# Routing's two small products ahead of image 0's last three w1 products, ternary and bias steps behind its weighted tiles

## The chip, the cores and the metric

The kernel runs on one core of a Trainium2 chip. The core has a matrix engine (PE, with its weight loads shown apart as PEld), a vector engine (DVE), an activation engine (ACT), a general engine (POOL), and a queue engine (SP) from which almost all transfers here are issued. Each engine works through its own instructions in order and waits on semaphores for the others. The metric is the device time of one execution in microseconds. Before the change the median of three runs was 3424.55 us, from 3424.52 to 3428.01 us. All data are float32.

## The reference, cut to what matters

Four layers are applied in turn to x of shape 8 x 384 x 32 x 32: a convolutional attention block, a gated mixture of four experts, a ternary depthwise and pointwise convolution, and a deformable attention block. The change touches the second layer and the preparation of the third layer's weights.

```
scores = softmax(x_flat @ gate_w + gate_b)         # 4 experts
top_v, top_i = top_k(scores, 2)
top_w = softmax(top_v)
wmap = top_w.T.reshape(K, b, h, w)                 # by position in the flat list
present = (top_i[:, :, None] == arange(e)).any(0)  # over all tokens
coef = einsum('ke,kbhw->ebhw', present, wmap)
hdn = relu(einsum('bchw,edc->ebdhw', x, w1) + b1)
y   = einsum('ebdhw,eod->ebohw', hdn, w2) + b2
out = einsum('ebohw,ebhw->bohw', y, coef)

# third layer: weights made ternary, then two convolutions
scale = 1 / max(mean(abs(w)), 1e-5)
u = clip(round(w * scale), -1, 1)
```

Which experts are present is a maximum over all tokens of all images, so nothing can be weighted before every token has been routed. The weighting is linear in one number per token: with w0 the first choice's weight, an expert's coefficient is dp x w0 + p1, where p1 says whether the expert is anybody's second choice, and dp is "anybody's first choice" less p1.

## The kernel before, in words

Each image is held as 128 partitions x 3 channel blocks x 1024 tokens and handled in two halves of 512 tokens. [...] a float32 product shows as two passes in the profile.

The stretch of interest lies between the first layer and the pipelined loop over images. There, image by image, the first layer's output is joined and the gate logits are accumulated (`logits`, L1239). Between these, PE takes the first products of layer 2 for image 0, whose list of units `layer1(pl, 0, True)` (called late) makes:

- 24 units of `hidden` (L1493): for each half and each of 12 hidden tiles, three products with w1; ACT then applies bias and relu (L1503) to a tile named hd (first half) or hx (second half). In the late form the tiles are not weighted at once.
- 24 units of `result`: for each half, each of 3 output blocks m and each of 4 parts, three products with w2 (L1514) that accumulate in one bank y. With the first four units (half 0, m = 0) go the weights of half 0's tiles, with the next four (half 0, m = 1) those of half 1's: ACT makes a coefficient tile cb from the broadcast weight w0s (L1475), and DVE multiplies each hidden tile by it (`weight`, L1479). After the last part DVE adds y to the image (L1520).
- The bias step (`bias`, L1466) adds w0 x yb to the image in three DVE operations per half; it is called ahead of the weights.

`route` (L1255 on) turns the logits by products with sel2 (L1263), has DVE and ACT work out the softmax, the two maxima, the presence pres and the weight w0 (L1272 to L1324), then takes all w1 units still left off the list, and then has PE do two small products: ppres sums pres over all partitions (L1313), and w0t turns w0 (L1327). DVE makes prs and w0r of them (L1317, L1329). w0r is stored to DRAM (w0d, L1330), from where `spread` loads it broadcast over all partitions (w0s, L1457). This load waits for the store. `coefficients` makes dp and yb.

`weights23` loads the third layer's weights pw2 and dw2 into raw (L1354, L1355), makes them ternary on DVE (tap2 small, upw2 128 x 1152), with one product pm on PE (L1380) that sums the magnitudes mp (L1378), and prepares two small vectors. It is called after the ninth result unit.

Order on an engine follows a scheduler, which may place an instruction ahead of others traced before it. `tc.issue_after(ins)` holds the instructions traced in its block behind `ins` on that engine. Before the change weights23 is held behind w0r's copy. Image 1's x loads (L171) and o loads (L1425) are issued from SP in the same stretch. Banks of PSUM for these products come from `fbank`, three in turn.

Of the kernel before, what the change touches and what calls it, by code (L numbers as in the profile page):

```python
# [9 lines left out]
ALU = mybir.AluOpType  # L10
# [4 lines left out]
P = 128  # L15
KC = C // P
# [17 lines left out]
NE = 4  # L34
# [21 lines left out]
def tile_kernel(ctx: ExitStack, tc: tile.TileContext, i: dict, out: bass.AP):  # L56
    nc = tc.nc
# [97 lines left out]
    def bn_moments(st, j, tiles):  # L155

        return nc.vector.bn_aggr(tiles[0][:, j, :], st[:, j, :, :].rearrange("p a b -> p (a b)"))
# [109 lines left out]
    with ExitStack() as pa:  # L267
# [46 lines left out]
        ident = const.tile([P, P], F32, name="ident_sb")  # L314
# [103 lines left out]
        first = [[w[0] for w in work].index(u) for u in range(NU0)]  # L418
# [103 lines left out]
        for n, (u, kind, s) in enumerate(work):  # L522
            k, h = divmod(u, 2)
# [19 lines left out]
            if n == len(work) - 2:  # L543
                spread = spread_qk()
# [8 lines left out]
            if kind == "v":  # L553
                h, c = h + s, 0
# [5 lines left out]
            for p in passes:  # L560
                j, x = p
                c0, c1 = max(0, 1 - x), W - max(0, x - 1)
                for q in range(nq):
# [3 lines left out]
                    elif kind == "y":  # L567
                        g, j, w = s, q, slice(0, 64)
# [103 lines left out]
    with ExitStack() as pb:  # L672
# [195 lines left out]
        for n, (b, pr, h, kc) in enumerate(steps):  # L868
# [49 lines left out]
            if kc == NT8 - NS:  # L918
                turned = normalise(b, pr, h, pav)
# [14 lines left out]
        for m in range(KC):  # L934
            first = bn_moments(ost, m, sc_o)
# [72 lines left out]
    with tc.If(redo > 0):  # L1008
        with ExitStack() as pb:
# [13 lines left out]
            with tc.For_i(0, B) as bi:  # L1023
# [44 lines left out]
                for pr in range(NPAIR0):  # L1068
                    qt, kt = qks[0][:, pr, :], qks[1][:, pr, :]
                    for h in range(2):  # L1070
                        pav = bank(f"pav_e{pr}_{h}")
                        for j, r in enumerate(HR):
                            hd = 2 * pr + j
# [73 lines left out]
    def load_w(name):  # L1147
        src = i[name]
        t = wd.tile(list(src.shape), F32, tag=name, name=name + "_sb")
        nc.sync.dma_start(out=t, in_=src)  # L1150
        return t
# [8 lines left out]
    def fbank(name):  # L1160
        return ps_f.tile([P, HALF], F32, tag="f", name=name)
# [93 lines left out]
    def route(units, end):  # L1255


        ls = pl.one([P, HALF], "ts", "ls")
        nc.vector.tensor_copy(ls, plog)

        pt = fbank("plt").rearrange("p (q a b e) -> p q a b e", q=8, a=2, b=B)
        for q in range(4):
            nc.tensor.matmul(  # L1263
                pt[:, q].rearrange("p a b e -> p (a b e)"), lhsT=ls[:, q * P : (q + 1) * P],
                rhs=sel2, start=True, stop=True,
            )
        nc.tensor.matmul(
            pt[:, 4, 0].rearrange("p b e -> p (b e)"), lhsT=ones,
            rhs=tb.rearrange("p b e -> p (b e)"), start=True, stop=True,
        )  # L1270
        gb = wd.tile([P, B, NE], F32, name="gb")
        nc.vector.tensor_tensor(  # L1272
            gb, pt[:, 4, 0], gbias.unsqueeze(1).to_broadcast([P, B, NE]), ALU.add
        )
        nt = B * NT8
        lg = pl.one([P, B, NT8, NE], "vt", "lg")
        for a in range(2):
            for q in range(4):
                nc.vector.tensor_tensor(lg[:, :, 4 * a + q, :], pt[:, q, a], gb, ALU.add)
        l = lg.rearrange("p b t e -> p (b t) e")  # L1280
        wk = pl.one([P, 3, nt, NE], "kt", "routing")
        wv = pl.one([P, 5, nt], "om2", "routed")

        def bc(ap):
            return ap.unsqueeze(2).to_broadcast([P, nt, NE])

        sc, eq, oh = (wk[:, k] for k in range(3))
        m = wv[:, 4]
        nc.vector.reduce_max(m, l, AX.X)
        nc.vector.tensor_tensor(l, l, bc(m), ALU.subtract)  # L1290
        nc.scalar.activation(sc, l, AF.Exp)
        nc.vector.reduce_sum(m, sc, AX.X)
        nc.vector.reciprocal(m, m)
        nc.vector.tensor_tensor(sc, sc, bc(m), ALU.mult)
        tops = []
        for k in range(2):
            mk, ek = wv[:, 2 * k], wv[:, 2 * k + 1]
            nc.vector.reduce_max(mk, sc, AX.X)

            nc.vector.tensor_tensor(eq, sc, bc(mk), ALU.is_equal)  # L1300
            nc.vector.tensor_tensor(
                eq, eq, ewt.unsqueeze(1).to_broadcast([P, nt, NE]), ALU.mult
            )
            nc.vector.reduce_max(ek, eq, AX.X)
            nc.vector.tensor_tensor(oh, eq, bc(ek), ALU.is_equal)
            nc.vector.reduce_max(pres[:, k, :], oh.rearrange("p t e -> p e t"), AX.X)
            if k == 0:
                nc.vector.scalar_tensor_tensor(sc, oh, -2.0, sc, ALU.mult, ALU.add)
            tops.append(mk)
        while len(units) > end:  # L1310
            units.pop(0)()
        pp_ = fbank("ppres")
        nc.tensor.matmul(  # L1313
            pp_[:, : 2 * NE], lhsT=ones, rhs=pres.rearrange("p k e -> p (k e)"),
            start=True, stop=True,
        )
        nc.vector.tensor_scalar(  # L1317
            prs.rearrange("p k e -> p (k e)"), pp_[:, : 2 * NE], 0.0, None, ALU.is_gt
        )
        nc.vector.tensor_tensor(m, tops[1], tops[0], ALU.subtract)  # L1320
        nc.scalar.activation(m, m, AF.Exp)
        nc.vector.tensor_scalar(m, m, 1.0, None, ALU.add)
        w0f = w0.rearrange("p b t -> p (b t)")
        nc.vector.reciprocal(w0f, m)  # L1324

        wt = fbank("w0t")
        nc.tensor.transpose(wt[:nt, :P], w0f, ident)  # L1327
        wr = pl.one([P, HALF], "ts", "w0r")
        routed = nc.vector.tensor_copy(wr[:nt, :P], wt[:nt, :P])  # L1329
        nc.sync.dma_start(out=w0_dram.rearrange("b (t p) -> (b t) p", p=P), in_=wr[:nt, :P])  # L1330
        return routed

    prs = wd.tile([P, 2, NE], F32, name="prs")
    dp = wd.tile([P, NE], F32, name="dp")
# [74 lines left out]
    ahead = {"time": 0.0}  # L1409
# [5 lines left out]
    def layer1(pl, b, late=False):  # L1415
# [11 lines left out]
        state = {}  # L1427
# [35 lines left out]
        def bias(h):  # L1463
            hs = slice(h * HALF, (h + 1) * HALF)
            for m in range(KC):
# [2 lines left out]
                    ALU.mult, ALU.add,  # L1468
                )

        def weight(h, k):
            e, dc = divmod(k, KC)
            if dc == 0:
                cb = state["cb"] = pl.one([P, HALF], "cb", f"cb{b}_{h}_{e}", 2)
                nc.scalar.activation(  # L1475
                    cb, state["w0", h], AF.Identity, bias=p1[:, e : e + 1], scale=dp[:, e : e + 1]
                )
            hd = state[h, k]
            nc.vector.tensor_tensor(hd, hd, state["cb"], ALU.mult)  # L1479

        def spare(k):

# [43 lines left out]
        units = []  # L1526

        def unit(*calls):
            units.append(lambda: [f(*a) for f, *a in calls])

        if late:
            for h in range(2):
                unit((enter, h), (hidden, h, 0))
                for k in range(1, NE * KC):
                    unit((hidden, h, k))
            for h in range(2):
                for m in range(KC):
                    for part in range(4):

                        w, n = (0, part) if h == m == 0 else (1, 4 * m + part - 4)  # L1540
                        first = []
                        if n == 0:
                            first += [(spread, w), (bias, w)]
                        if h == 0 and n < 4:
                            first += [(weight, w, 3 * n + k) for k in range(3)]
                        unit(*first, (result, h, m, part))
            return units
        spread(0)
# [616 lines left out]
    units = layer1(pl, 0, True)  # L2165
# [4 lines left out]
    for b in range(1, B):  # L2170
# [8 lines left out]
        if b + 2 == B:  # L2179
            with tc.issue_after(ahead["load"].ins):  # L2180
# [1 line left out]
                wq3, wk3, wv3, wp3 = (load_w(n) for n in ("wq3", "wk3", "wv3", "wp3"))  # L2182
                pb3, dw3, bn3, pw3 = (load_w(n) for n in ("pb3", "dw3", "bn3", "pw3"))
                ref3, npos, half3, same = (load_w(n) for n in ("ref3", "npos", "half3", "same"))
    routed = route(units, 2 * NE * KC)
    coefficients()
    with pd:
        for k, u in enumerate(units):
            u()
            if k == 8:  # L2190
                with tc.issue_after(routed.ins):
                    tap2, upw2, mp, so3, bo3, sum2, edge2 = weights23(pl)
        def layers(b):
            xt = xs_img.pop(b)
            yield from layer2(pl, b, xt)
            yield from layer3(pl, b, xt, put_image(b), False)

        for b in range(B - 1):
            units = layer1(pl, b + 1)
            due = 0.0  # L2200
            this = layers(b)
            for idle in this:
                if idle is None:
                    if b == B - 2:
                        break
                    continue
                due += idle
                while due >= UNIT and units:
                    units.pop(0)()
                    due += ahead["time"] - UNIT  # L2210
                    ahead["time"] = 0.0
            if b == B - 2:
                for _ in range(5):
                    next(this)
            for u in units:
                u()

        def fill(n):
            for _ in range(n):
                next(this, None)  # L2220

        for _ in last_image(pl, xs_img.pop(B - 1), fill):
            pass
        in_range(slice((B - 2) * NU3, B * NU3), 1)
        okm = pl.one([P, 1], "okm", "okm3")
        nc.vector.tensor_reduce(okm, oks, AX.X, ALU.min)
        pok = fbank("pok3")
        nc.tensor.matmul(pok[:, 0:1], lhsT=ones, rhs=okm, start=True, stop=True)
        nc.vector.tensor_scalar(bad3, pok[:, 0:1], P - 0.5, None, ALU.is_lt)
# [164 lines left out]
```

## Time and profile before

| What | Value |
|---|---|
| Median of three runs | 3424.55 us |
| Profiled execution: its own time | 3426.77 us |
| Profiled execution: span | 3424.7 us |
| PE busy | 3325.3 us (97%) |
| DVE busy | 1776.0 us (52%) |
| ACT busy | 1300.0 us (38%) |
| POOL busy | 203.7 us (6%) |
| w1 products, PE, L1493 | 1104 recorded, 597 ns each |
| w2 products, PE, L1514 | 1080 recorded, 599 ns each |
| cb, ACT, L1475 | 797 to 815 ns each |
| weighted tiles, DVE, L1479 | 684 ns each |
| mean granted PE clock | 0.989 |

A row of the profile names the line, the engine, the operation, and the tiles written and read. "<-" in a wait names what ended it. Matmuls overlap, so the start-to-start time, about 0.43 us a pass in this stretch, tells PE's rate better than the duration of one. Times of a stretch are us from the start of the span. The granted clock is a share of full speed; half rate is 0.50.

### The profile page before, as it was taken

The page shows a single profiled execution, that of the slowest core. Times are in us where ns is not written, and L with a number is a line of the kernel's source. Part 1 is how long each engine was busy: PE and PEld are TensorE (multiplying, and loading weights), DVE is VectorE, ACT ScalarE, POOL GpSimd, SP SyncE. Part 2 cuts the span into 40 slices and gives each one's busy share as a digit, 9 for nine tenths or more (in the row PEclk, how much of TensorE's full clock was granted, in tenths as well). Part 3 has the DMA queues.
Part 4 walks back from the last instruction along what each step waited for, and adds up shares of the span by engine and source line. Part 5 has one row for each costly group of instructions (what it writes and reads, how often), then busy time and mean ns, then how long its engine had stood idle before and what let it go on. Part 6 is the DMA issues. An engine that isn't in the chain of part 4 may idle for free.

```text
span 3424.7 us, 44837 instructions
## 1 busy us (share of the span) xinstructions
PE 3325.3 (97%) x18479; PEld 1440.2 (42%) x18479; DVE 1776.0 (52%) x2982; ACT 1300.0 (38%) x1519; POOL 203.7 (6%) x237
## 2 busy tenths in 40 slices
PE   6999999999999999999889999999999999999989
PEld 2443434343434343434334444444444444444444
DVE  8852232323232323234456586565855658658765
ACT  5655444444444444434212332223322232222341
POOL 2110000000000000000000110201102011020121
PEclk9999999999999999999899999999999999999999
DMA  9972121212121211112810110101101011010000
GB/s 354 295 226 81 27 80 27 81 26 80 27 73 34 65 43 58 50 57 63 304 41 22 36 40 26 60 28 36 40 30 56 28 36 40 36 55 23 0 19 38
DMA packets 86980, 234.56 MB, mean 68 GB/s; under 512 B 21881, under 2 KB 22105, under 8 KB 79851
## 3 DMA queue, kind: packets, MB, share of 16 engines
q1 hardware_dynamic: 84602, 223.30, 20.3%
q10 hardware_dynamic: 1248, 4.72, 0.4%
q8 instruction: 149, 2.44, 0.3%
q0 software_dynamic: 912, 3.53, 0.3%
q14 instruction: 69, 0.56, 0.1%
HBM read 146.33 MB, written 75.59 MB: 65 GB/s over the span
## 4 chain that ended last, share of the span: by engine, by line
PE 49%; DVE 1%; DMA 1%; ACT 0%; POOL 0%; issue 0%; SPq 0%; DVEq 0%; POOLq 0%; ACTq 0%
PE ph L1493 15%; PE y L1514 14%; PE pf L2022 4%; PE pq L1674 3%; PE pw L1645 3%; PE pav L1894 3%; PE s L1868 2%; PE pk L1839 1%; DVE off L1770 1%; PE pv L1850 1%; PE xsb L1820 1%; PE pw_last L2083 1%; PE xs L1820 0%; PE px L1734 0%; PE plog L1239 0%; PE pom L1701 0%
## 5 line engine op out<-in xcount | busy, mean ns | idle before, releaser
L827 ACT ACTIVATE p<-s 128x1024 f32<-128x1024 f32 x512 | 496.3, 1021 | 365.7 <-PE s L820 365.5
L1493 PE MATMUL ph<-h,w_sb 128*128 128x512 f32 x1104 | 487.9, 597 | 14.7 <-DMA b_sb<-in_b_dram 14.6
L1514 PE MATMUL y<-hd,w_sb 128*128 128x512 f32 x1080 | 487.4, 599 | 11.1 <-DVE hd L1479 11.1
L835 PE MATMUL pav<-p,vt 64*64 64x512 f32 x4096 | 494.7, 588 | 0.0
L820 PE MATMUL s<-qk,qk 48*64 48x512 f32 x2944 | 355.2, 592 | 0.0
L1493 PEld LDWEIGHTS ph<-h,w_sb 128*128 128x128 f32 x1104 | 208.4, 191 | 272.3 <-issue 269.8
L1514 PEld LDWEIGHTS y<-hd,w_sb 128*128 128x128 f32 x1080 | 200.0, 191 | 242.7 <-issue 222.6
L796 DVE COPY ta<-pav 128x512 f32<-128x512 f32 (+1 forms) x65 | 44.2, 682 | 475.5 <-PE pav L835 475.5
L835 PEld LDWEIGHTS pav<-p,vt 64*64 64x64 f32 x4096 | 168.3, 133 | 273.7 <-issue 273.4
L1503 ACT ACTIVATE hd<-ph,b_sb 128x512 f32<-128x512 f32 x180 | 122.6, 681 | 265.1 <-PE ph L1493 265.1
L574 PE MATMUL pk<-xs,cws_sb 32*32 32x496 f32 (+3 forms) x3840 | 182.9, 614 | 37.8 <-DMA xs<-in_xs_dram 24.6
L1770 DVE SCALAR_TENSOR_TENSOR off<-q,dw_sb,off 128x225 f32<-128x225 f32 (+4 forms) x441 | 215.3, 541 | 2.6
L1633 DVE SCALAR_TENSOR_TENSOR y<-h,tap,y 128x961 f32<-128x961 f32 (+1 forms) x168 | 202.9, 1227 | 0.5
L820 PEld LDWEIGHTS s<-qk,qk 48*64 48x64 f32 x2944 | 109.4, 133 | 211.2 <-issue 190.3
L81 DVE COPY qk<-pq 128x512 f32<-128x512 f32 x46 | 31.8, 691 | 251.9 <-PE pq L258 251.9
L1885 ACT ACTIVATE p<-s 128x1024 f32<-128x1024 f32 x96 | 93.4, 1021 | 162.0 <-PE s L1868 152.6
L1479 DVE TENSOR_TENSOR hd<-hd,cb 128x512 f32<-128x512 f32 x180 | 122.2, 684 | 37.8 <-ACT hd L1503 37.5
L574 PEld LDWEIGHTS pk<-xs,cws_sb 32*32 32x32 f32 (+1 forms) x3840 | 78.8, 112 | 140.4 <-issue 57.3
L1954 POOL TENSOR_TENSOR p<-p,p 128x1024 f32<-128x1024 f32 x48 | 113.6, 2367 | 325.9 <-ACT p L1885 267.1
L2022 PE MATMUL pf<-att,wp_sb 128*128 128x512 f32 x288 | 131.3, 601 | 0.0
L820 PE MATMUL s<-ql,ql 48*64 48x512 f32 x1024 | 128.2, 592 | 0.2 <-ACT p L827 0.2
L711 PE MATMUL pv<-wv_sb,g 128*128 128x384 f32 x384 | 127.1, 489 | 0.0
(369 smaller groups left out, 3745.2 us busy)
## 6 DMA issues: line engine op xcount, KB each, us to landing
rqk<-y SPq DMA_DIRECT2D x96, 256.0 KB
g<-rqk SPq DMA_DIRECT2D x96, 256.0 KB
xs<-in_xs_dram SPq DMA_DIRECT2D x56, 384.0 KB
g<-rv SPq DMA_DIRECT2D x48, 256.0 KB
xh<-in_x_dram SPq DMA_DIRECT2D x48, 256.0 KB
f<-in_x_dram SPq DMA_DIRECT2D x24, 512.0 KB
f<-o SPq DMA_DIRECT2D x24, 512.0 KB
o<-ot SPq DMA_DIRECT2D x42, 256.0 KB
```

What stands on the lines that cost most here:

```text
L574: nc.tensor.matmul(banks[r][cols[q]].rearrange("p (h w) -> p h w", w=W)[:, :, c0:c1], lhsT=cws[rs, c, 2 * h + g, x, w], rhs=src[rs, :, c0 ...
L711: nc.tensor.matmul(pv[:, :C], lhsT=acts[b][2][:, c, t * P : (t + 1) * P], rhs=w_in[2][:, c, :], start=(c == 0), stop=(c == KC - 1),)
L820: nc.tensor.matmul(s[64 * k : 64 * k + 64, j * HALF : (j + 1) * HALF], lhsT=kt[r, k0 : k0 + 64], rhs=qt[r, h * HALF : (h + 1) * HALF], sta ...
L827: nc.scalar.activation(p, s, AF.Exp, scale=scale)
L835: nc.tensor.matmul(pav[k][64 * j : 64 * j + 64, :], lhsT=vts[b % 2][r, kc, 2 * hd : 2 * hd + 2, :].rearrange("p a b -> p (a b)"), rhs=p[r, ...
L1479: nc.vector.tensor_tensor(hd, hd, state["cb"], ALU.mult)
L1493: ahead["ph"] = nc.tensor.matmul(ph, lhsT=w1[:, e, c, dc * P : (dc + 1) * P], rhs=state["h1"][c], start=(c == 0), stop=(c == KC - 1),)
L1503: nc.scalar.activation(hd, ph, AF.Relu, bias=b1[:, k : k + 1])
L1514: nc.tensor.matmul(y, lhsT=w2[:, e, dc, m * P : (m + 1) * P], rhs=state[h, k], start=(k == 0), stop=(k == NE * KC - 1),)
L1633: nc.vector.scalar_tensor_tensor(d, f, tap2[:, c, t : t + 1], d, ALU.mult, ALU.add)
L1770: nc.vector.scalar_tensor_tensor(d, f, dw3[:, t : t + 1], d, ALU.mult, ALU.add)
L2022: nc.tensor.matmul(pf, lhsT=wp3[:, pr, m * P : (m + 1) * P], rhs=att[:, pr, hs], start=(pr == 0), stop=(pr == NPAIR3 - 1),)
```

## The change

One edit is on PE's order and two are on DVE's. In `route`, the loop that takes the remaining w1 units stops three units short; these three come after the turning product w0t, held behind it on PE. In the late units of image 0, `bias` goes from the head of the first part to a call `late_bias` after the weights of the fourth part, held behind the last weighted tile so far. `weights23` is held behind the last weighted tile traced when it is called, not behind w0r's copy.

```diff
-        while len(units) > end:
+        while len(units) > end + 3:
             units.pop(0)()
         pp_ = fbank("ppres")
...
-        nc.tensor.transpose(wt[:nt, :P], w0f, ident)
+        turned = nc.tensor.transpose(wt[:nt, :P], w0f, ident)
         wr = pl.one([P, HALF], "ts", "w0r")
-        routed = nc.vector.tensor_copy(wr[:nt, :P], wt[:nt, :P])
+        nc.vector.tensor_copy(wr[:nt, :P], wt[:nt, :P])
         nc.sync.dma_start(out=w0_dram.rearrange("b (t p) -> (b t) p", p=P), in_=wr[:nt, :P])
-        return routed
+        with tc.issue_after(turned.ins):
+            while len(units) > end:
+                units.pop(0)()
...
+        def late_bias(h):
+            with tc.issue_after(ahead["hd"].ins):
+                bias(h)
...
-            nc.vector.tensor_tensor(hd, hd, state["cb"], ALU.mult)
+            ahead["hd"] = nc.vector.tensor_tensor(hd, hd, state["cb"], ALU.mult)
...
                         if n == 0:
-                            first += [(spread, w), (bias, w)]
+                            first += [(spread, w)]
                         if h == 0 and n < 4:
                             first += [(weight, w, 3 * n + k) for k in range(3)]
+                        if n == 3:
+                            first += [(late_bias, w)]
                         unit(*first, (result, h, m, part))
...
-    routed = route(units, 2 * NE * KC)
+    route(units, 2 * NE * KC)
...
-                with tc.issue_after(routed.ins):
+                with tc.issue_after(ahead["hd"].ins):
                     tap2, upw2, mp, so3, bo3, sum2, edge2 = weights23(pl)
```

On the SP queue the order changes with it. Before: pw2, dw2 and two of image 1's three x loads, then the store of w0d, the third x load, and the broadcast load w0s. After: the store of w0d, pw2, w0s, dw2, and then the three x loads.

## The prediction

> **What bounds the kernel now.** I read the page's busy shares first: PE is busy for 3325.3 of 3424.7 us (97%), DVE for 52%, ACT for 38%. So PE's own stream sets the time, and a change can gain only what PE idles or runs slowly. The view of waits, for PE, from 1700 us to the end, lists where PE still waits (columns: waiting engine and line, what it waited for, us in total, times, longest us):
>
> ```profile
> PE y L1514 <- DVE hd L1479: 11.1, 1, 11.1
> PE pav L1894 <- DVE tu L1966: 5.4, 1, 5.4
> PE pw_last L2083 <- ACT y_last L2075: 3.3, 1, 3.3
> ```
>
> The first line is one single wait, the largest left after 1700 us, and it lies exactly where the diff edits. To see what fills it I took the chain that ended last, in order of time, for 1680 to 1800 us (start, duration, what):
>
> ```profile
> 1702.43 18.11 PE ph L1493 x42
> 1720.54 0.14 PE ppres L1313 x2
> ...
> 1720.69 0.17 DVE prs L1317
> 1720.86 0.26 DVE w0r L1329
> ...
> 1721.53 2.43 DMA w0d<-w0r
> ...
> 1724.03 5.12 DMA w0s<-w0d
> ...
> 1729.17 2.08 DVE f L1466 x3
> 1731.25 0.61 DVE hd L1479
> ...
> 1731.91 25.45 PE y L1514 x54
> ```
>
> PE runs all its w1 products, then the two small products (ppres, w0t). Only then can the routing weight go through DRAM: copy w0r, store w0d, broadcast load w0s, bias steps, first weighted tile hd. All that time PE has nothing. Was the input of the small products ready earlier? The timeline of instructions answers:
>
> ```profile
> 1712.37 0.51 DVE L1306 TENSOR_REDUCE pres<-routing 128x4 f32<-128x256 f32 x1
> 1712.65 1.02 PE L1493 MATMUL ph<-h,w_sb 128*128 128x512 f32 x2
> 1720.37 0.28 PE L1313 MATMUL ppres<-pres,ones 128*128 128x8 f32 x2
> 1720.57 0.69 ACT L1503 ACTIVATE hx<-ph,b_sb 128x512 f32<-128x512 f32 x1 [1.83 <-PE ph L1493]
> ```
>
> pres was complete at 1712.88 and w0's reciprocal (L1324) at 1712.45. The matmul at 1712.65 is the first of the last three w1 units. So the products waited 7.5 us behind three units that do not need them.
>
> The wait has a second price. The table by stretches (columns: stretch, length, busy us and count of PE, PEld, DVE, ACT, POOL, then granted clock, DMA share, GB/s) shows PE's clock falling during it:
>
> ```profile
> 1724.00:1725.00 1.00, 0.00 (x0) 0.00 (x0) 0.93 (x9) 0.00 (x0) 0.00 (x0) 1.00 0.72 287
> 1727.00:1728.00 1.00, 0.00 (x0) 0.00 (x0) 0.00 (x0) 0.00 (x0) 0.00 (x0) 0.50 0.83 336
> 1730.00:1732.00 2.00, 0.09 (x1) 0.10 (x1) 2.00 (x4) 0.77 (x2) 0.00 (x0) 0.50 0.00 0
> ```
>
> The clock records put the half rate at 1725.74 to 1735.98 us. The y products therefore start slowly: 54 passes took from 1731.91 to 1757.19, or 25.28 us. At the 0.4287 us a pass of the w1 stream (1712.65 to 1720.37 holds 18) they need 23.15. Lost: 2.13 us.
>
> [...] half rate starts 4.9 us after PE stopped and lasts 10.24 us. [...] Here the 32 KB store took 2.43 us, [...] the trace shows cb behind the last hx on ACT, and I use that below.
>
> **The change part by part.** The clock starts at 1712.65, where PE is ready for the first of the last three units.
>
> (1) Products ahead of the last three units. They wait for pres: 1712.88 plus 0.05 (hd's end to PE's load at 1731.9 took that). From ppres to the end of prs took 1720.86 - 1720.37 = 0.49; with a weight load ahead, some 0.6. In the changed program's order the next w1 product takes ppres's PSUM bank and so waits for prs. I put its start at 1713.6, that is 0.95 late. Of this, 0.42 (1720.37 to 1720.79) is the products' own time, paid before too. New PE loss: 0.53. Bounds: 0.2 and 1.2. Behind this wait on PE stand only the three units. They end at 1713.6 + 18 x 0.4287 = 1721.32.
>
> (2) The DRAM chain. w0r ended 0.74 after ppres began, so now at about 1713.05 + 0.74 = 1713.8. From w0r's end (1721.11) to cb's start (1729.26) the path took 8.15, so w0s is usable at 1721.95. On the SP queue two things change. The 576 KB load of pw2 was far ahead; now it is issued between w0d and w0s. It replaces a 512 KB load of x in the same place, so I take the same time. The rest of image 1's x and dw2 go behind w0s, and x is first used near 1791, some 65 us later. Bounds of the chain: 0.5 us faster, 3 us slower if pw2 and x's loads share the engines with w0s worse than x did.
>
> (3) ACT. cb stands behind the last hx. PE's end to hx's end was 1720.37 to 1721.26 = 0.89, so hx ends at 1722.21. That is later than w0s's 1721.95: the two nearly tie, and ACT decides. cb starts at 1722.25 and takes 0.81.
>
> (4) Bias moved behind the weighted tiles. The first hd no longer waits for three L1466 steps. They ended at 1731.25 while cb was ready near 1730.07, so this alone is worth 1.1 us. Now hd: 1723.06 + 0.05 + 0.68, and y starts at 1723.84. PE idles 1723.84 - 1721.32 = 2.52 us. The bias is then needed by y's first addition (L1520), about 10 us after y starts, while DVE needs 7.3 + 2.1 us for twelve hd and three bias steps: no wait on PE, as the bank y leaves is one of three.
>
> (5) Ternary steps moved behind the weighted tiles. Before, the small ones lay in DVE's idle time (1721.1 to 1726.2), costing nothing; now neither, with one cover to watch: pm on PE, the sum of pw2's magnitudes, stands after 54 y passes, at 1723.84 + 23.15 = 1747.0, and needs mp (1.33 us). DVE reaches mp after 24 weights (about 14.7 us), six bias steps (4.2), one y addition (0.75) and a 0.17 reduction: 1723.1 + 19.8 + 1.33 = about 1744.3. Slack 2.7 us. The large steps (upw2, some 5 us) follow pm as before, long ahead of the first use in image 0's pointwise product.
>
> (6) [...] the half rate should not come: 2.13 us saved.
>
> Sum: before 11.12 + 2.13 = 13.25 lost; after 0.53 + 2.52 = 3.05. Gain 10.2 us. After this stretch the order on every engine is the same, and PE is at 100% from 1800 to 3200 (0.06 to 0.22 us missing in some stretches), so what PE gains it keeps. The profiled execution took 3426.77, which would become 3416.6; the median of the three runs is 3424.55, which becomes 3414.4. Those runs spread over 3.5 us, one at 3428.01; [...] I allow 2 us either way.
>
> **The rivals.** R1, a late transfer takes the wait over: w0s comes 2 to 4 us later since pw2 lies ahead of it. For: its slack against ACT is 0.3 us, and w0s's packets were already slow (5.12 us for 512 KB). Against: x's load lay in the same place before. The gap becomes about 5.3 us at 3 us late, the clock can fall again, and the gain shrinks to 5.5 to 7.5: 3417.0 to 3419.1. R2, the gain is given back at image 1's start: PE waited only 0.88 there (ph after h L1443), but its o loads are issued only when image 0's last y products free buffers. If those loads had a fixed time, 3424.5. Against: that issue is tied to PE's own progress and moves with it. R3, slower: pm. If DVE reached mp late, PE, in order, would stand before it with the y products behind. It costs from 2.7 us of lateness on, and the kernel is slower once DVE is over 2.7 + 10.2 = 13 us late, for example 20 us late: 3431.7. For: mp now stands behind some 20 us of DVE work. Against: the durations are measured and DVE is idle for 4.6 and 8.8 us in that stretch before.
>
> **How the numbers follow.** About 0.2% (6.85 us, 3417.7) is what a measurement can tell from no change. Forecast 0.83, with its own range 3412 to 3417; R1 0.10, half of it beyond 3417.7; R2 0.04; R3 0.03. Faster 0.83 + 0.05 = 0.88, same 0.05 + 0.04 = 0.09, slower 0.03. The range runs from 1's best bound with a favourable tail, 3411.6, to most of R1, 3418.6.
>
> **What would show it.** Right: ppres near 1713, PE's wait before y at 2 to 3 us and put down to hd, no half-rate record there, y starting near 1723.8, pm with no wait. Wrong: cb starting well after the last hx, released by w0s (R1); a wait before pm (R3); a larger wait at ph or x of image 1 (R2); or PE idling over 1.2 us before ppres.

## The result, and the profile after

The changed kernel took 3416.61 us (median of 8 runs, 3414.96 to 3421.18). The kernel before, run beside it, took 3427.31 us (8 runs, 3424.52 to 3430.43). The medians lie 10.7 us apart. The ratio is 0.9971, with the interval 0.996 to 0.9982, which is 9.9 us of the whole.

The profiled execution of the changed kernel is the slowest of its eight: 3421.18 us, with a span of 3419.1 us. Its span is only 5.6 us shorter than before's 3424.7. So I cut both profiles at two points, the start of the logits' copy ls (L1259, shortly ahead of the edit) and the first normalisation product gna_d of image 1 (L117, behind it):

| Piece | Before | After | Difference |
|---|---|---|---|
| start of span to ls | 1700.32 us | 1704.23 us | +3.91 |
| ls to gna_d of image 1 | 99.75 | 90.08 | -9.67 |
| gna_d to the end | 1624.63 | 1624.80 | +0.17 |

The 3.91 us lie ahead of everything that the change touches. In the fourteen profiles of this study ls starts anywhere from 1697.98 to 1706.27 us, while the piece from gna_d to the end takes 1623.69 to 1625.48. So the spread between runs comes mostly from the start. Below I therefore give times from ls, not from the start of the span.

In the view of waits for PE, from 1700 us to the end, the wait before y is no longer the largest (waiting engine and line, what it waited for, us in total, times, longest us):

```profile
PE pav L1902 <- DVE tu L1974: 5.4, 1, 5.4
PE pw_last L2091 <- ACT y_last L2083: 3.1, 1, 3.1
PE y L1520 <- DVE hd L1485: 2.2, 1, 2.2
...
PE ppres L1313 <- DVE pres L1306: 0.2, 1, 0.2
```

The old 11.1 us line is now 2.2, and a new, small one stands ahead of ppres. The chain that ended last, in order of time, shows the new order (start, duration, what):

```profile
1716.36 0.44 DVE pres L1306
1716.80 0.14 issue
1716.93 0.37 PE ppres L1313 x2
1717.33 0.18 DVE prs L1317
...
1717.55 8.01 PE ph L1499 x18
...
1725.62 0.54 issue
1726.17 0.81 ACT cb L1481
...
1727.00 0.70 DVE hd L1485
...
1727.75 23.44 PE y L1520 x54
1751.19 0.12 PE pm L1382 x2
```

In this profile no DMA is on the chain of this stretch any more: PE's three w1 units (18 passes) cover the DRAM path, and after them comes ACT's cb. The 54 passes of y take 23.44 us instead of 25.45. The table by stretches shows the clock (stretch, length, busy us and count of PE, PEld, DVE, ACT, POOL, then granted clock, DMA share, GB/s):

```profile
1726.00:1728.00 2.00, 0.25 (x1) 0.25 (x2) 1.00 (x2) 1.67 (x3) 0.00 (x0) 1.00 1.02 414
1728.00:1730.00 2.00, 2.00 (x6) 0.80 (x5) 2.00 (x4) 0.81 (x1) 0.00 (x0) 1.00 0.47 182
```

PE idles in the first of these, but the clock stays at 1.00, where before it was 0.50 behind the gap.

### The profile page after: what moved, and what is told of

Its sections match the earlier page's. It is cut to its first block, busy times and chain, and to the rows that moved or that the text cites. A ratio compares the mean times of both kernels' runs of the same rounds, so it can differ in the third digit from the quotient of the medians.

```text
span 3419.1 us, 44835 instructions
## 1 busy us (share of the span) xinstructions
PE 3321.6 (97%) x18479; PEld 1440.5 (42%) x18479; DVE 1776.3 (52%) x2982; ACT 1299.8 (38%) x1519; POOL 204.1 (6%) x237
## 4 chain that ended last, share of the span: by engine, by line
PE 49%; DVE 2%; ACT 0%; DMA 0%; POOL 0%; issue 0%; DVEq 0%; SPq 0%; POOLq 0%; ACTq 0%
PE y L1520 14%; PE ph L1499 14%; PE pf L2030 4%; PE pq L1682 3%; PE pw L1653 3%; PE pav L1902 3%; PE s L1876 2%; PE pk L1847 1%; DVE off L1778 1%; PE pv L1858 1%; PE xsb L1828 1%; PE pw_last L2091 1%; PE xs L1828 0%; PE px L1742 0%; PE plog L1239 0%; PE pom L1709 0%
```

## The experiments

A single time of the whole kernel varies by several us for the reason given above. The gain is therefore read from the stretch between ls and pm (the product after 54 y passes). All columns are us. "Half rate" is the clock record in this stretch that shows 0.50: its start after ls, and its length.

| Kernel | ppres starts | PE waits before y | y starts | pm starts | y to pm | Half rate | Image 1's first product |
|---|---|---|---|---|---|---|---|
| before | 20.06 | 11.12 | 31.59 | 56.88 | 25.29 | 25.42, 10.24 long | 95.73 |
| after | 12.70 | 2.20 | 23.52 | 46.80 | 23.28 | none | 85.65 |
| after, again | 12.71 | 2.65 | 23.96 | 47.24 | 23.28 | none | 86.09 |
| e_order | 12.70 | 3.65 | 24.95 | 49.93 | 24.98 | 25.37, 3.41 long | 88.78 |
| e_cover | 20.05 | 10.03 | 30.50 | 55.82 | 25.32 | 24.40, 10.24 long | 94.67 |
| e_warm | 20.05 | 1.15 | 31.45 | 54.73 | 23.28 | none | 93.58 |
| e_bias_back | 12.71 | 3.49 | 24.81 | 49.65 | 24.85 | 24.58, 3.41 long | 88.50 |
| e_tern_back | 12.70 | 2.79 | 24.09 | 49.07 | 24.98 | 25.05, 3.41 long | 87.92 |
| e_two | 14.91 | 3.80 | 24.66 | 49.64 | 24.97 | 25.33, 3.41 long | 88.49 |
| e_four | 12.70 | 0.25 | 23.74 | 47.02 | 23.28 | none | 85.87 |
| e_mp_late | 12.70 | 2.38 | 23.69 | 54.67 (68 passes) | 30.98 | 24.45, 3.41 long | 87.51 |
| e_first | 12.70 | 2.20 | 23.52 | 46.80 | 23.28 | none | 85.64 |
| e_cb_dve | 12.69 | 1.75 | 23.05 | 46.30 | 23.25 | none | 85.15 |
| e_best | 12.70 | none | 23.72 | 46.90 | 23.18 | none | 85.75 |

In e_best ls itself comes one w1 unit earlier; it is compared by another mark below.

### The parts alone, and the clock by itself

**e_order** is the kernel before with the order of PE's work changed, and nothing else.

```diff
-        while len(units) > end:
+        while len(units) > end + 3:
             units.pop(0)()
...
-        nc.tensor.transpose(wt[:nt, :P], w0f, ident)
+        turned = nc.tensor.transpose(wt[:nt, :P], w0f, ident)
...
+        with tc.issue_after(turned.ins):
+            while len(units) > end:
+                units.pop(0)()
         return routed
```

> The kernel before with the order of PE alone changed: the two small products ahead of the last three w1 units; bias steps and ternary steps stay where they were. I measure the stretch from the start of ls (L1259) to the first pass of pm: 56.87 us before, 46.80 after. My theory: the order of PE carries nearly all. PE's wait before y is 1.1 us longer than after (2.2 to about 3.3 us) since three bias steps stand ahead of the first weighted tile; the stretch is 47.9 us and the time some 9 us under before. Rival 1, the covering steps on DVE carry the gain: the stretch is 54 us or more. Rival 2, the 3.3 us gap already brings the half clock rate: the stretch is 49.5 us or more.

Measured: 3419.05 us (11 runs, 3417.94 to 3425.79), ratio 0.9976, interval 0.9967 to 0.9985. pm comes 6.95 us earlier than before, against 10.08 with all three edits. The chain that ended last shows what the other edits add:

```profile
1721.80 6.67 DMA w0s<-w0d
...
1728.49 2.08 DVE f L1469 x3
1730.57 0.61 DVE hd L1482
...
1731.23 25.14 PE y L1517 x54
```

The three bias steps (f) still stand between the broadcast load and hd, the gap before y is 3.65 us, and one piece at half rate, 3.41 us, comes back.

**e_cover** is the other half: PE's order as before, bias and ternary steps behind the weights.

```diff
-            nc.vector.tensor_tensor(hd, hd, state["cb"], ALU.mult)
+            ahead["hd"] = nc.vector.tensor_tensor(hd, hd, state["cb"], ALU.mult)
...
-                            first += [(spread, w), (bias, w)]
+                            first += [(spread, w)]
...
+                        if n == 3:
+                            first += [(late_bias, w)]
...
-                with tc.issue_after(routed.ins):
+                with tc.issue_after(ahead["hd"].ins):
```

> The kernel before with bias and ternary steps behind the weighted tiles, the products still behind all w1 units. My theory: this is worth only the 1.1 us of the bias steps; PE's wait before y falls from 11.1 to about 10.0 us, the half rate still comes, and the stretch from ls to pm is 55.8 us. Rival, the ternary steps did stand in the way of the routing weight: 53 us or less.

Measured: 3426.38 us (12 runs), ratio 0.9998, interval 0.9989 to 1.0006. The waits of PE in this stretch:

```profile
PE y L1518 <- DVE hd L1483: 10.0, 1, 10.0
```

This is 11.1 less the 1.1 us of the bias, and the whole stretch is 1.06 us shorter. The kernel's time can't tell this from nothing. So the two halves bring 6.95 and 1.06 us alone, and 10.08 together. Of the missing 2.07 us, 1.70 is the half rate that e_order still has (24.98 us from y to pm against 23.28); the other 0.37 comes from cb, which starts 0.36 us later behind a slower load of w0s (6.67 us against 5.78).

**e_warm** measures the clock alone: before, with eleven products of extra work that fill PE's wait. Nothing is left out; their result is not used.

```diff
+        with tc.issue_after(turned.ins):
+            warm = fbank("warm")
+            for k in range(11):
+                nc.tensor.matmul(
+                    warm, lhsT=w1[:, 1, 0, :P],
+                    rhs=w1[:, 0].rearrange("p c n -> p (c n)")[:, :HALF],
+                    start=(k == 0), stop=(k == 10),
+                )
```

> The kernel before with eleven products on w1 put into PE's idle time behind w0t, into a bank that nobody reads (extra work, 9.4 us). It takes away the half clock rate and nothing else. My theory: y starts at the same time after ls as before and then runs at full rate, so the stretch from ls to pm is 2.1 us shorter than before, 54.7 us. Rival, the slow y passes come from DVE's weighted tiles and not from the clock: the stretch stays at 56.9 us.

The chain that ended last has the same y row as the kernel before, at another length:

```profile
1729.43 23.44 PE y L1522 x54
```

y starts nearly where it did before (31.45 against 31.59 us after ls), and pm comes 2.15 us earlier. The passes of y make 2.01 of this (25.29 to 23.28): the price of the half rate, 2.13 in the prediction. The other 0.14 is y's earlier start. Measured: 3422.1 us (20 runs), ratio 0.9986, interval 0.9979 to 0.9992, that is 2.7 to 7.2 us of the whole. The stretch explains 2.15 of it; the rest is not explained.

### One edit undone

**e_bias_back** is the changed kernel with the bias steps at their old place.

```diff
-                            first += [(spread, w)]
+                            first += [(spread, w), (bias, w)]
...
-                        if n == 3:
-                            first += [(late_bias, w)]
```

> The kernel after with the bias steps put back at the head of the first part; ternary steps stay behind the weighted tiles. My theory: PE's wait before y grows by 1.1 us to 3.3 us, and the stretch from ls to pm is 47.9 us against 46.8. Rival, the routing weight's transfer decides and the bias steps do not matter: 46.8 us.

Measured: pm at 49.65, that is 2.41 to 2.85 us behind the two runs of the changed kernel; 3419.03 us in one run. The wait before y:

```profile
PE y L1520 <- DVE hd L1485: 3.5, 1, 3.5
```

y starts 0.85 to 1.29 us later, which is the bias (1.1 us) give or take the load's time, and half rate adds 1.57 us behind the longer gap. So the same edit is worth 1.06 us with the old order, where PE's clock is lost in any case, and more than twice that in this one run with the new order.

**e_tern_back** is the changed kernel with the ternary steps held behind w0r's copy, as before.

```diff
-        nc.vector.tensor_copy(wr[:nt, :P], wt[:nt, :P])
+        routed = nc.vector.tensor_copy(wr[:nt, :P], wt[:nt, :P])
...
-                with tc.issue_after(ahead["hd"].ins):
+                with tc.issue_after(routed.ins):
```

> The kernel after with the ternary steps held behind w0r's copy again, as before the change. On DVE the magnitude sum mp and the first reduction m then stand ahead of the first weighted tile, and wait for the loads of pw2 and dw2, which SP now issues around w0s. My theory: both loads have landed by the time cb is ready, so nothing changes: stretch from ls to pm 46.8 us. Rival: dw2's load, queued behind w0s, is later than cb and holds up DVE, and PE with it: 47.5 us or more.

Measured: pm at 49.07; one run took 3418.72 us. Yet DVE was not in the way: hd follows cb by 0.85 us, as in the changed kernel. What differs is the load of w0s, at 6.89 us the longest of all runs. It made the gap 2.79 us, and half rate followed for 3.41 us. By stretches:

```profile
1724.00:1726.00 2.00, 2.00 (x4) 0.86 (x4) 2.00 (x5) 0.82 (x1) 0.00 (x0) 0.67 0.24 93
1726.00:1728.00 2.00, 2.00 (x3) 0.68 (x2) 2.00 (x5) 0.82 (x1) 0.00 (x0) 0.50 0.01 3
```

PE is busy throughout both rows, but at 0.67 and 0.50 of its clock. The edit on the ternary steps is not shown to be worth anything by itself; whether it changes how long w0s takes, one run can't say.

### What limits the new order

**after, again** is the changed kernel without an edit, to see how far its own profile repeats.

> The kernel after, unchanged, for comparison on the same chip. Stretch from ls to pm 46.8 us; the time about 10 us under before.

Measured: 3417.54 us (7 runs, 3415.5 to 3423.14), ratio 0.9973, interval 0.9962 to 0.9984. The chain that ended last differs from that of the first profile:

```profile
1716.52 6.77 DMA w0s<-w0d
...
1723.39 0.82 ACT cb L1481
```

Here the load of w0s, 6.77 us instead of 5.78, ends last, and ACT has been free for 0.2 us. So ACT and the transfer nearly tie, and either can decide. By the chain, the transfer decided here and in e_order, e_bias_back, e_tern_back, e_two and e_four.

**e_two** and **e_four** put two or four w1 units behind the small products, not three.

```diff
-        while len(units) > end + 3:
+        while len(units) > end + 2:
```

> The kernel after with two w1 units behind the small products in place of three. My theory: PE no longer waits for pres, but the routing weight's way through DRAM starts 2 us later than it could and covers less: y starts 25.8 us after ls, PE waits some 5.4 us, [...] the half rate comes back and the stretch from ls to pm is 50 to 51.5 us against 46.8. Rival: only the sum of waits counts and no clock is lost: 48.5 to 49.1 us.

> The kernel after with four w1 units behind the small products. My theory: PE comes to the products 2.6 us too early and waits for pres some 2.9 us; the wait before y stays at 2.2 to 2.5 us because cb stands behind the last hx on ACT; [...] Stretch from ls to pm 49.5 us against 46.8. Rival: the fourth unit fills the wait before y, and it comes out even: 47 us.

Measured: with two, ppres starts 2.21 us later and the whole DRAM path with it; the gap is 3.80 us and half rate returns for 3.41 us. pm is at 49.64 (one run: 3420.30 us). With four, pm is at 47.02 (one run: 3417.57 us), as good as three. My theory missed what the order would be: cb was placed ahead of the last hx on ACT, so the fourth unit filled the wait instead of delaying cb. PE's waits moved to the other side of the products:

```profile
PE ppres L1313 <- DVE pres L1306: 2.8, 1, 2.8
...
PE y L1520 <- DVE hd L1485: 0.2, 1, 0.2
```

The fourth unit covers nothing new, since PE now runs out of work before pres is ready. The version at the end, e_best, moves both sides together.

**e_cb_dve** makes the first coefficient tile on DVE, so that it doesn't queue behind hx on ACT.

```diff
-                nc.scalar.activation(
-                    cb, state["w0", h], AF.Identity, bias=p1[:, e : e + 1], scale=dp[:, e : e + 1]
-                )
+                if late and h == e == 0:
+                    nc.vector.tensor_scalar(
+                        cb, state["w0", h], dp[:, e : e + 1], p1[:, e : e + 1], ALU.mult, ALU.add
+                    )
+                else:
+                    nc.scalar.activation(
+                        cb, state["w0", h], AF.Identity, bias=p1[:, e : e + 1], scale=dp[:, e : e + 1]
+                    )
```

> The kernel after with only the first cb tile made on DVE. It shows when w0s has landed, with ACT out of the way. My theory: ACT decided by a little; cb starts within 0.7 us before or at +21.9 us after ls, takes about half as long on DVE, and PE's wait before y falls from 2.2 to 1.0 to 1.8 us; the stretch from ls to pm is 45.7 to 46.5 us. Rival: the broadcast load is the limit, as in the two runs with products ahead and bias at the head (landed 22.2 after ls): wait of 2 us or more.

Measured: the gap is 1.75 us and pm at 46.30, 0.50 to 0.94 us better than the changed kernel. cb took 0.55 us on DVE, against 0.81 on ACT, and now it waits for the load of w0s. One run took 3419.26 us, which says nothing at this size.

**e_first** issues the loads of pw2 and dw2 behind that of w0s on the SP queue, to test whether pw2 makes w0s late.

```diff
-        nc.sync.dma_start(out=pw2, in_=i["pw2"])
-        nc.sync.dma_start(out=dw2, in_=i["dw2"])
+        with tc.issue_after(ahead["w0s"].ins):
+            nc.sync.dma_start(out=pw2, in_=i["pw2"])
+            nc.sync.dma_start(out=dw2, in_=i["dw2"])
...
-                nc.sync.dma_start(
+                ahead["w0s"] = nc.sync.dma_start(
```

> The kernel after with the loads of pw2 and dw2 queued on SP behind the broadcast load w0s, not ahead of it and right behind it; image 1's x loads follow as before. The four other runs with the products ahead took 6.5 to 6.9 us for w0s (5.8 in the profile of after), the orders without that 5.0 to 5.3. My theory: pw2's 576 KB ahead of w0s costs the difference; w0s now takes 5.0 to 5.4 us, ACT decides again, PE's wait before y is 2.2 us, and the stretch from ls to pm is 46.8 us. Rival: the 1.5 MB of x loads behind w0s cost it, pw2 does not matter: w0s 6.3 us or more and a wait of 2.4 us or more.

On SP's queue w0s now goes ahead of pw2 (start, duration, line, what):

```profile
1715.67 0.34 SPq L1460 DMA_DIRECT2D w0s<-w0d  x1
1716.05 0.42 SPq L1357 DMA_DIRECT2D raw<-in_pw_dram  x1
```

Measured: w0s took 4.17 us from issue to landing, less than the theory's 5.0 to 5.4 and less than in any other run. The stretch is that of the first profile (pm at 46.80; one run: 3415.6 us), because ACT decides again: w0s landed 19.68 us after ls, but cb, behind the last hx, started at 21.94. The x loads still follow w0s, so the rival is refuted in this run.

From issue to landing w0s took:

| Ahead of w0s on the queue | Runs | us |
|---|---|---|
| a load of x (old order) | before, e_cover, e_warm | 5.12, 5.28, 4.99 |
| pw2 (new order) | the changed kernel twice, e_order, e_bias_back, e_tern_back | 5.78, 6.77, 6.67, 6.52, 6.89 |
| pw2 (new order) | e_mp_late, e_four, e_two, e_best, e_cb_dve | 6.49, 6.55, 5.34, 5.43, 6.09 |
| neither | e_first | 4.17 |

(The expectation names four runs at 6.5 to 6.9 us; there were six, and three shorter ones.) The packets agree. In the ten runs with pw2 ahead, its packets of 4608 bytes run until 2.2 to 2.4 us after w0s is issued, and the first packet of 4096 bytes, w0s's size, starts 1.57 to 1.90 us after the issue. In e_first that packet starts after 0.97 us, and pw2's packets follow from 2.84 us on. So pw2 ahead makes w0s 1.2 to 2.7 us slower, by one run against ten. In the kernel before, a load of x took that place.

This gain is hidden behind ACT here. In e_cb_dve, where ACT is out of the way, y starts 1.47 us after w0s has landed. With e_first's landing at 19.68 that would be 21.15 us after ls, ahead of the end of the last w1 pass at 21.31. By this estimate the two edits together close the gap; they were not run together.

**e_mp_late** is the changed kernel with the reduction mp done seven times, so that pm would have to wait for it (extra work).

```diff
-        nc.vector.tensor_reduce(mp, pw2, AX.XY, ALU.add, apply_absolute_value=True)
+        for _ in range(7):
+            nc.vector.tensor_reduce(mp, pw2, AX.XY, ALU.add, apply_absolute_value=True)
```

> The kernel after with the magnitude sum mp worked out seven times over on DVE, 7.6 us more work ahead of pm. It prices the slower rival of the prediction. My theory: mp ended 3.5 us before PE came to pm, so PE waits for the rest, 4.1 us, and the stretch from ls to pm is 50.9 us against 46.8. Rival: DVE has idle time in front of mp that absorbs it: under 48 us.

The chain that ended last:

```profile
1723.23 31.15 PE y L1521 x68
1754.38 0.12 PE pm L1383 x2
```

Before pm stand 68 y passes, not 54. The order on PE had been moved when DVE's work grew, and PE never waited for mp. The theory missed, and the price of a late mp has not been measured. One run took 3417.97 us.

### A version that beats both

**e_best** takes e_cb_dve, four units behind the small products, and one unit fewer ahead of the last logits.

```diff
-        while len(units) > end + 3:
+        while len(units) > end + 4:
...
-        for _ in range(3 if b > 3 and b % 2 else 2):
+        for _ in range(3 if b == 5 else 2):
```

(The edit of e_cb_dve is in it too.)

> The kernel after with two more edits: one w1 unit fewer ahead of the last logits products and four units, not three, behind the two small products; and the first coefficient tile cb of half 0 made on DVE, so that it does not stand behind the last hx on ACT. My theory: the 2.2 us that PE still waits before y is all there is to have; PE does not wait before the last logits, the four units cover the routing weight's way through DRAM, and y starts right behind them. From the start of the third group of logits products to y's first pass it takes 40.2 us, against 42.15 after and 50.22 before; to pm 63.4 (65.43, 75.51). Rival: PE then waits for image 7's join ahead of the last logits products, or for a slower broadcast load, and it is 42 us or more.

Measured: 3414.14 us (5 runs, 3408.91 to 3414.46), before 3426.33, ratio 0.9955, interval 0.9941 to 0.9968. The changed kernel on the same chip had 0.9973, 0.9962 to 0.9984. The chain that ended last:

```profile
1711.40 0.37 PE ppres L1313 x2
...
1712.02 10.57 PE ph L1504 x24
1722.59 23.18 PE y L1525 x54
1745.77 0.12 PE pm L1382 x2
```

y follows the w1 units with no gap and no other engine between. From the start of the third group of logits, a mark that the moved unit doesn't shift, pm comes after 62.96 us; the changed kernel needs 65.43 and 65.88, before 75.51. So 2.5 to 2.9 us more are won. The intervals of the whole kernel overlap, but all five runs of e_best lie below the fastest of the changed kernel's seven beside them (3415.5 us). With no gap, no half rate shows in this stretch, and y to pm takes 23.18 us.

## Why the prediction was right

The mechanism that the prediction names is the one that the runs show: the products ahead (e_order), the bias behind (e_cover) and the full clock (e_warm). Step 2 came out right by luck, and step 6 was an estimate that no trace of before shows and that other runs contradict. The third edit, on the ternary steps, is not shown to be worth anything by itself (e_tern_back).

Predicted were 3414.4 us as the median, in a range of 3412 to 3417, and a gain of 10.2 us. The median is 3416.61, inside that range; against the eight-run median of before, 3427.31, the gain of 10.2 would have given 3417.1. In the stretch the gain is 10.08 us at pm (56.88 to 46.80 after ls) and at image 1's first w1 product (95.73 to 85.65).

- **Step 1, the products wait for pres.** Right: the next unit starts 0.99 us late (0.95 predicted), with 0.21 of waiting at ppres. New loss 0.57, predicted 0.53.
- **Step 2, the DRAM chain.** The sum was right in the first profile, but by luck, as two errors offset each other. From w0r's end to w0s's landing took 7.76 us, before 8.04. The store w0d was quicker, 1.83 against 2.43, and issued 0.36 us sooner, but the load was slower, 5.78 against 5.12. So the store's 2.43 us are not a fixed time: the same 32 KB took 2.25 to 2.43 in the three runs of the old order and 1.83 to 1.86 in six of the new (after, again, e_order, e_bias_back, e_tern_back, e_two). "So I take the same time" failed as a rule: over the ten runs with pw2 ahead of w0s, the path took 7.32 to 8.88 us, and 6.16 in e_first. Rival 1's mechanism is there, at up to 1.9 us over the old order rather than 2 to 4.
- **Step 3, ACT decides, in a near tie.** Right, also in its second half: cb starts 0.90 us after the pass that would have come next on PE (1717.55 + 18 x 0.4287 = 1725.27), predicted 0.93. That it was ACT holds for the first profile; in six other runs, after again among them, the transfer came last.
- **Step 4, the bias.** Right for the gap: 1.06 us (e_cover), and 2.48 us of gap from that same point to y's start at 1727.75, predicted 2.52. (The wait's 2.2 counts from the last pass's end, 0.28 later.) Too small as the worth of the edit: by e_bias_back, one run, it is 2.4 to 2.9 us, because the longer gap (3.49 us) also brings 3.41 us of half rate.
- **Step 5, the ternary steps.** pm had no wait: mp ended at 1747.52 and pm started at 1751.03, a slack of 3.5 us against 2.7. e_tern_back shows no DVE work in hd's way, as step 5 says of before.
- **Step 6, the clock.** The outcome was right in both profiles of the changed kernel, 23.28 us for y against 23.15, and e_warm gives the saving as 2.01 us. That a gap of 2.52 us would not bring half rate was the author's estimate, and it does not hold: gaps of 2.38 (e_mp_late) and 2.79 us (e_tern_back) did bring it. At 2.20 and 2.65 us the changed kernel kept full rate. The 2.65 us put no more than 1.66 into one piece of the clock's records, while all 2.38 of e_mp_late lay in one (last section); where the piece began was luck.
- **Rival 2, the gain given back at image 1.** Nearly nothing: 10.08 us at image 1's first product, 9.67 at its gna_d. Image 1's second o load took 4.87 us instead of 4.17, and the x step behind it starts 6.68 us after the first o load's issue instead of 5.98. The half-rate record there starts at 1794.88, behind gna_d (1794.31), so it has no part in this. From pm to gna_d the thirteen profiles with 54 passes take 42.47 to 43.28 us, and 0.41 lies within that. Rival 3 is untested, as pm never waited in any run.

## What to carry to other kernels

When a long chain hangs on a small product, put it on PE as soon as its input is ready, and count the independent work behind it on both sides: too few units leave a gap (e_two: 3.80 us), too many move the wait ahead of the product (e_four: 2.8 us at ppres). Look at the last link before the wait ends, as a coefficient on a busy engine's queue can be cheaper elsewhere (e_cb_dve: 0.55 us on DVE, 0.81 on ACT). Keep large loads that nobody waits for out of the queue ahead of a small one that the chain needs (e_first, one run: 4.17 us for w0s, against 5.34 to 6.89 behind pw2). And close a short gap on PE entirely if it can be done: in the runs here, a gap of 2.4 to 3.8 us cost up to 1.7 us more through the clock.

## What was not expected of the hardware

In the profiles of before and of the changed kernel, the half-rate records that end inside the span are 3.41, 6.83, 10.24, 23.89 and 27.31 us long. All bounds of clock records inside the span lie on one grid of 3413.33 ns in each of the two (a third of 10.24 us), to within 0.01 us. Its place relative to the program differs between runs: in the stretch studied half rate, where it came, began 24.40 to 25.42 us after ls. So I count in pieces of 3.41 us; where no half-rate record is near, I count them on from one further off.

In before, PE idled through a whole piece, 1722.33 to 1725.74, and half rate followed. In the experiments a piece in which PE idled only in part was enough:

| PE idle in the piece of 3.41 us | Kernel | Next piece |
|---|---|---|
| 3.27, 2.99, 2.75, 2.45, 2.38 us | e_bias_back, e_order, e_two, e_tern_back, e_mp_late | half rate |
| 2.02, 1.94, 1.66, 1.54, 1.13 us | e_four, e_first, after again, before (the start of its long wait), after | full rate |
| 1.42 us (at the start of image 1) | after | half rate |

In the stretch studied, then, none of the pieces listed with up to 2.02 us of idle time was followed by half rate, and each of those from 2.38 us on was. The last row, with less idle time than four of the row above, shows that idle time alone doesn't decide: that piece also holds small products of the normalisation (gna_d, 0.38 us from 1794.31). Around it, the stretches of the changed kernel are:

```profile
1794.88:1798.29 3.41, 3.41 (x7) 1.46 (x6) 1.24 (x6) 0.72 (x1) 0.55 (x1) 0.50 0.02 5
1791.47:1794.88 3.41, 1.99 (x6) 0.82 (x6) 2.90 (x6) 1.38 (x2) 0.00 (x0) 1.00 0.00 0
```

PE was busy for 1.99 of 3.41 us in the second row, and the piece after it (the first row) ran at 0.50. One half-rate piece, filled by PE, cost 1.7 us here: y to pm is 24.98 instead of 23.28 us. What exactly the clock counts stays open.
